# Moving small VectorE and GpSimd steps to other hooks of a Strassen-Winograd block kernel, and one row's load ahead of other transfers

## The chip, the cores and the metric

The kernel runs on one core of one Trainium2 chip. The metric is device time in microseconds (us) of one execution; the figure of a kernel is the median of its runs. TensorE (PE) multiplies matrices into PSUM, VectorE (DVE), ScalarE (ACT) and GpSimd (POOL) do the elementwise work, and SyncE (SP) issues most transfers. Each engine works through its own queue in the order in which the program issued the instructions, and waits on semaphores for the others.

## The reference

The input `x` is 2 x 2048 x 512 in float32, with one condition vector of 512 for each of the two batches. Cut to what matters:

```python
emb = jnp.dot(jax.nn.silu(t), ada_w) + ada_b
shift_msa, scale_msa, gate_msa, shift_mlp, scale_mlp, gate_mlp = jnp.split(emb, 6, axis=-1)
norm = _ln(x) * (1.0 + scale_msa[:, None]) + shift_msa[:, None]
h = jax.nn.gelu(jnp.dot(norm, ssm_w1) + ssm_b1, approximate=False)
x = x + gate_msa[:, None] * (jnp.dot(h, ssm_w2) + ssm_b2)
norm2 = _ln(x) * (1.0 + scale_mlp[:, None]) + shift_mlp[:, None]
hf = jax.nn.gelu(jnp.dot(norm2, ff_w1) + ff_b1, approximate=True)
x = x + gate_mlp[:, None] * (jnp.dot(hf, ff_w2) + ff_b2)
```

`_ln` is a layer norm without weights. `ssm_w1` and `ssm_w2` are 512 x 512, `ff_w1` is 512 x 1024, `ff_w2` is 1024 x 512. There are two residual branches, and each is two matrix products.

## The kernel before, in words

**Tiling.** The 4096 tokens are cut into 8 blocks of 512 tokens (blocks 0 to 3 are the first batch, 4 to 7 the second). A block `x_i` lies in SBUF as 128 partitions of 4 tokens (`C = 4`) with 512 features each, so most elementwise instructions are 128x512.

**Products.** Each block needs the products hA (first layer of the ssm branch), oA (its second layer), hC (first layer of the feed-forward branch, in two groups 0 and 1) and oC (its second layer). Each is done as seven products of half-size quarters, P1 to P7, in the form of Strassen and Winograd: sums of quarters of both operands are made beforehand (`sums_of_first`, `sums_of_second`, lines 212 to 215 and 222 to 225), and the results are put together in three PSUM tiles, the banks y, x and v. P1, P6, P7 and P4 accumulate in y, P2 in x, P5 and P3 in v. After each product VectorE reads what has been accumulated so far, into `s1`, `u2` and `s5` for a first layer (lines 452 to 466; the gelu follows on ScalarE, lines 447 and 470), or straight into the residual `x` for a second layer (line 498). The next product that accumulates in the same bank has to wait for that read. The usual order is

```python
ORDER = ("P1", "P2", "P6", "P5", "P7", "P3", "P4")
```

hA_0 has an order of its own, P1, P2, P5, P6, P3, P7, P4, and oA_0 and hA_1 have `FIRST`, which is P1, P2, P5, P6, P7, P3, P4.

**Hooks.** There is no scheduler: the queue of each engine is the order in which the Python code runs. `group` (line 272) issues the matmuls of a product, then what `after` does with it, then the operations hooked to that product:

```python
            for op in hooks.get(p, ()):
                op()
```

`hook(hooks, places, ops)` hangs the n-th operation on the n-th place, and all further ones on the last place. Which product an operation is hooked to thus settles what stands before and behind it in the queue of its engine.

**The steps that the change touches.** A layer norm is, per token, `bn_stats` and `bn_aggr` on VectorE (lines 324 and 325, one pair for each of the four c), then eight small instructions on GpSimd that make `rstd` and `nmr` (`scales`, lines 333 to 351), then four ScalarE instructions (`normal`, line 364). The result must be turned, features to partitions: blocks 0 and 1 do it with TensorE transposes (`pt`, line 393), the later ones with four VectorE transposes of 32x32 blocks (`turn`, line 375) and 16 transfers from SBUF to SBUF (`move`, line 384). Scale and shift of the condition follow on ScalarE (line 407) or VectorE (line 409).

The gates are folded into the second weights: `make_gate` puts a gate row on all partitions of a PSUM tile (`pgate`, line 201), and `weight_of_second` multiplies `w2` (4 instructions) or `fw2` (8 instructions) by it on VectorE (line 255), with four sums on GpSimd behind them. In `fold2(lo, hi)` the numbers 0 to 3 are the folds of `w2`, and 4 to 7 are its sums. The second bias is multiplied by the gate (`gb2_0`, line 641, and for the second batch line 517) and added to `x` by GpSimd in four instructions (`biases`, line 510). The bias row itself comes by a transfer that SP issues (`load_row`, line 122), 256 KB since it is copied to all 128 partitions, into one of two buffers.

**Around the change.** In the first group (hA_0, oA_0, hA_1) the weights are folded while the first products run. At the batch switch, in block 3 of the loop, the gate of the feed-forward branch is made anew for batch 1 (`refold5`). In the last block but one (`early`, i = 6) oA_7 is put ahead of the second group of hC_6, and the norm of block 7 (`norm_2`) is hooked to the products of that group.

Of the kernel before, what the change touches and what calls it, by code (L numbers as in the profile page):

```python
# [43 lines left out]
def kernel(  # L44
# [16 lines left out]
    nc = tc.nc  # L61
# [9 lines left out]
    PER_B = N // TB  # L71
# [49 lines left out]
    def load_row(t, row):  # L121
        nc.sync.dma_start(out=t, in_=row.unsqueeze(0).to_broadcast([P, D]))
        return t
# [23 lines left out]
    b2_bc = work.tile([P, D], F32, tag="gb", name="gb2_0", bufs=2)  # L147
# [34 lines left out]
    def rows_of_gates(g):  # L182

        pa = ps_g.tile([P, D], F32, tag="x", name=f"pada_{g}")
        for k in range(KD):
            nc.tensor.matmul(
                pa[k * G : (k + 1) * G, :],
                silu[:, k, :],
                ada[g][:, k, :],
                start=True,  # L190
                stop=True,
                tile_position=(0, k * G),
            )
        r = work.tile([P, D], F32, tag="grows", name=f"grows_{g}", bufs=2)
        nc.vector.tensor_tensor(r, pa, brows[:, (2, 5).index(g), :], ALU.add)
        gate_rows[g] = r
# [105 lines left out]
    def hook(hooks, places, ops):  # L302

        for n, op in enumerate(ops):
            hooks.setdefault(places[min(n, len(places) - 1)], []).append(op)
# [201 lines left out]
    def biases(i, gb):  # L507

        return [
            lambda c=c: nc.gpsimd.tensor_tensor(xs[i][:, c, :], xs[i][:, c, :], gb, ALU.add)  # L510
            for c in range(C)
        ]

    def gate_bias(g, b, row, name):

        t = load_row(work.tile([P, D], F32, tag="gb", name=name, bufs=2), row)
        return t, lambda: nc.vector.tensor_tensor(t, gate[g, b], t, ALU.mult)

    def store(i, half):
        s = slice(half * C // 2, (half + 1) * C // 2)  # L520
        nc.sync.dma_start(out=out_blk[i][:, s, :], in_=xs[i][:, s, :])
# [38 lines left out]
    def run(ops):  # L560
        for op in ops:
            op()
# [4 lines left out]
    n1 = {0: Norm(0, 1), 1: Norm(1, 1)}  # L567
# [61 lines left out]
    n1_sums = n1[0].summed(nc.vector)  # L629
# [3 lines left out]
    gb, hA = {2: b2_bc}, {}  # L633
# [9 lines left out]
    def fold2(lo, hi):  # L643
        return [lambda k=k: found["w2"][1][k]() for k in range(lo, hi)]

    hooks = {}
    hook(hooks, ("P1",), n1_sums[2:3])
    hook(hooks, ("P2",), [lambda: rows_of_gates(2)] + n1_sums[3:])
    st = n1[1].stats()
    hook(hooks, ("P5",), [ssm_gate] + fold2(0, 2))  # L650
    hook(hooks, ("P6",), [gb2_0] + biases(0, b2_bc) + fold2(2, 7))
    hook(hooks, ("P3", "P3", "P7"), st)
    hook(hooks, ("P7",), [lambda: modulation(3, 0)])
    hA[0] = First(0, n1[0].ops, hooks, ("P1", "P2", "P5", "P6", "P3", "P7", "P4"))
    w2_ops = found["w2"][0]
# [2 lines left out]
    hooks = {}  # L658
# [5 lines left out]
    st = n2[0].stats()  # L664
# [1 line left out]
    residual("oA_0", 0, hA[0], w2_ops, KD // 2, hooks, order=FIRST)  # L666
    fw1_ops, fw1_sums = weight_of_first("fw1", fw1_sb)
    run(fw1_sums)
    run(n1[1].summed(nc.vector))

    hooks = {}
    hook(hooks, ("P1",), st[2:] + [n2[0].scales])
    hook(hooks, ("P2",), [lambda c=c: n2[0].normal(c, on_pe=True) for c in range(C)])
    hook(hooks, ("P2",), biases(1, gb[2]))
    hook(hooks, ("P6",), [lambda: rows_of_gates(5)])
    hook(hooks, ("P3", "P3", "P4", "P4"), n2[0].turned((1, 3)))
    hA[1] = First(1, n1[1].ops, hooks, FIRST)
# [12 lines left out]
    def fold5(lo, hi):  # L690
        return [lambda k=k: found["fw2"][1][k]() for k in range(lo, hi)]
# [11 lines left out]
    for i in range(NBLK):  # L703
        nxt, nx2, last = i + 1 < NBLK, i + 2 < NBLK, i + 1 == NBLK
        if nx2:
            n1[i + 2] = Norm(i + 2, 1)

        hooks = {} if i else first_hooks
        if nxt:
            hook(hooks, EARLY if i else ("P2",), hA[i + 1].summed(nc.gpsimd))  # L710
        if nx2:
            hook(hooks, ("P2", "P3", "P4"), n1[i + 2].stats())
        if fold:
            hook(hooks, ("P5", "P7"), fold[:2])
        hC = Second(i)
        hC.group(0, n2[i].ops, hooks)

        def second_group(hooks):

            if nx2:  # L720
                hook(hooks, ("P1",), [n1[i + 2].scales])
                hook(hooks, EARLY, [lambda c=c: n1[i + 2].normal(c) for c in range(C)])
                hook(hooks, ("P7", "P3", "P3", "P4"), [lambda c=c: n1[i + 2].turn(c) for c in range(C)])
                hook(hooks, ("P4",), [n1[i + 2].move])
            if i == 0:
                hook(hooks, ("P1", "P2", "P6", "P5"), fold5(4, 8))
                hook(hooks, ("P7",), fold5(8, 12) + [gb5_0] + biases(0, gb[5]))
            if fold:
                hook(hooks, EARLY, fold[2:6])
            hC.group(1, n2[i].ops, hooks)  # L730

        def ssm_residual(hooks):

            if nx2:
                hook(hooks, ("P7",), n1[i + 2].moved())
            if fold:
                hook(hooks, EARLY, fold[6:8])
                hook(hooks, ("P7",), fold[8:])
            n2[i + 1] = Norm(i + 1, 2)
            st = n2[i + 1].stats()  # L740
            hook(hooks, ("P3", "P4"), st[:2] if early else st)
            late_stats.extend(st[2:] if early else ())
            residual(f"oA_{i + 1}", i + 1, hA[i + 1], w2_ops, KD // 2, hooks)

        def norm_2(hooks, turns, then):

            hook(hooks, ("P1",), late_stats + [n2[i + 1].scales])
            hook(hooks, ("P1",), [lambda c=c: n2[i + 1].normal(c) for c in range(C)])
            hook(hooks, turns, [lambda c=c: n2[i + 1].turn(c) for c in range(C)])
            hook(hooks, (then,), [n2[i + 1].move])  # L750


        early = nxt and not nx2
        late_stats = []
        hooks = {}
        hook(hooks, EARLY, hC.summed(0, nc.gpsimd))
        if early:
            ssm_residual(hooks)
            hooks = {}
            norm_2(hooks, ("P6", "P6", "P5", "P7"), "P7")  # L760
        second_group(hooks)
        if i == 0:
            fw2_ops = found["fw2"][0]
        hooks = {}
        hook(hooks, ("P1", "P1", "P1", "P2") if early else EARLY, hC.summed(1, nc.gpsimd))
        if nx2:
            ssm_residual(hooks)
            hooks = {}
        elif not nxt:
            for p in EARLY:  # L770
                run(hooks.get(p, ()))
            hooks = {}
        fold = None

        if nx2:
            norm_2(hooks, ("P2", "P2", "P6"), "P6")
        if i + 3 < NBLK:
            hook(hooks, ("P6",), [lambda: load_x(i + 3)])
        refold2 = (i + 2) % PER_B == 0 and nx2
        if refold2:  # L780
            b = (i + 2) // PER_B
            gb[2], multiply_2 = gate_bias(2, b, b2, f"gb2_{b}")
            hook(hooks, ("P1",), [lambda: load_w("w2", w2, w2_sb)])
        if nx2:
            if refold2:
                hook(hooks, ("P1",), [lambda: make_gate(2, b)])
                hook(hooks, ("P6",), [multiply_2])
            hook(hooks, ("P1", "P2"), n1[i + 2].summed(nc.gpsimd))
            hook(hooks, ("P6",) if refold2 else ("P2", "P6"), biases(i + 2, gb[2]))
        if nxt:  # L790
            hook(hooks, ("P5" if early else "P3",), n2[i + 1].moved())
        if early:
            hook(hooks, ("P7", "P7", "P3", "P3"), n2[i + 1].summed(nc.vector))
        hook(hooks, ("P3",), [lambda: store(i, 0)])
        residual(f"oC_{i}", i, hC, fw2_ops, KH // 2, hooks, last)
        if not last:
            store(i, 1)
        if nx2:
            run(n2[i + 1].summed(nc.gpsimd))

        refold5 = (i + 1) % PER_B == 0 and nxt
        if refold5:
            b = (i + 1) // PER_B
            gb[5], multiply = gate_bias(5, b, fb2, f"gb5_{b}")
            load_w("fw2", fw2, fw2_sb)
            make_gate(5, b)
            fw2_ops, fold = weight_of_second(fw2_sb, fw2_s, gate[5, b], (nc.vector,))
        hooks = {}
        if refold5:
            hook(hooks, ("P6",), [multiply])  # L810
        if nxt:
            hook(hooks, ("P6",) if refold5 else EARLY, biases(i + 1, gb[5]))
        if refold2:
            w2_ops, w2_fold = weight_of_second(w2_sb, w2_s, gate[2, b], (nc.vector,))
            hook(hooks, ALL, w2_fold)
        if nx2:
            hA[i + 2] = First(i + 2, n1[i + 2].ops, hooks)
        else:
            for p in ORDER:
                run(hooks.get(p, ()))  # L820
# [45 lines left out]
```

## Time and profile before

| | us |
|---|---|
| median of 3 runs | 621.32 (619.77 to 621.38) |
| the profiled execution, whole | 618.58 |
| its span, first to last instruction | 616.8 |
| TensorE busy | 603.8 (98%) |
| VectorE busy | 299.3 (49%) |
| ScalarE busy | 173.6 (28%) |
| GpSimd busy | 343.6 (56%) |

The granted clock of TensorE was 1.000 throughout. A line of the timeline or of a group gives start and length in us, engine, source line, operation and operands (out<-in); in brackets is the time for which the engine had been idle, and what ended it. Starts count from the first instruction of the span. A line of the waits gives the engine that waited and the tile it was about to write, with its source line, the instruction waited for, the sum of the waits in us, how many there were and the longest. TensorE's busy time takes in pipelining, so a group of 8 matmuls is shown with 1.89 us and the next one starts 1.73 us after it. The profiled execution is one of several, so its own time is the one that steps in the trace add up to.

### The profile page before, as it was taken

To read this page: it belongs to the slowest core of one execution; us is meant where nothing else is said; L and a number is where in the kernel's file an instruction comes from. 1 tells how busy PE (TensorE), PEld (TensorE's weight loads), DVE (VectorE), ACT (ScalarE), POOL (GpSimd) and SP (SyncE) were. 2 spreads that over 40 slices of the span, in tenths; PEclk is the share of its full clock that TensorE was granted. 3 is DMA by queue.
4 is the path that set the end of the run, shared out by engine and by line. 5 is a ranking of instruction groups with operands and counts; after the bars stand their busy time and mean duration, and the time that the engine had idled before them with its cause. 6 is when DMAs were issued, how large, how long until landed. Compare 5 with 4: busy or idle time off the path is not lost.

```text
span 616.8 us, 7847 instructions
## 1 busy us (share of the span) xinstructions
PE 603.8 (98%) x2899; PEld 523.3 (85%) x2899; DVE 299.3 (49%) x512; ACT 173.6 (28%) x259; POOL 343.6 (56%) x360
## 2 busy tenths in 40 slices
PE   6999999999999999999999999999999999899997
PEld 4777888888888888888888888888888888788886
DVE  4967775335552355534653357533555233714321
ACT  2233341142331431332421334214233141220110
POOL 2696489765543853539637466966654394160330
PEclk9999999999999999999999999999999999999999
DMA  8962002240113302360021820224011400021001
GB/s 323 413 254 69 1 8 62 56 149 1 33 37 95 111 1 69 94 180 17 2 68 39 241 81 13 56 56 149 1 43 27 131 7 2 0 69 68 1 2 69
DMA packets 22075, 47.74 MB, mean 77 GB/s; under 512 B 4068, under 2 KB 4624, under 8 KB 21140
## 3 DMA queue, kind: packets, MB, share of 16 engines
q1 hardware_dynamic: 21952, 47.20, 24.4%
q8 instruction: 23, 0.38, 0.3%
q14 instruction: 16, 0.13, 0.1%
q10 hardware_dynamic: 84, 0.03, 0.0%
HBM read 25.20 MB, written 8.39 MB: 54 GB/s over the span
## 4 chain that ended last, share of the span: by engine, by line
PE 89%; DMA 3%; DVE 3%; POOL 2%; issue 1%; ACT 1%; SPq 0%; DVEq 0%; POOLq 0%; ACTq 0%
PE py_oC L287 18%; PE py_hC L287 17%; PE pv_oC L287 9%; PE pv_hC L287 9%; PE py_oA L287 9%; PE py_hA L287 6%; PE pv_oA L287 5%; PE px_oC L287 4%; PE px_hC L287 4%; PE pv_hA L287 3%; PE px_oA L287 2%; DMA ada<-in_L_cond_ada_w_dram 2%; PE px_hA L287 1%; DMA gb<-in_L_cond_ff_b_dram 1%; PE pt L393 1%
## 5 line engine op out<-in xcount | busy, mean ns | idle before, releaser
L407 ACT ACTIVATE nT<-nT,mod,mod 128x512 f32<-128x512 f32 x52 | 38.1, 802 | 171.7 <-DMA nT<-blocks 159.7
L510 POOL TENSOR_TENSOR x<-x,gb 128x512 f32<-128x512 f32 x64 | 79.2, 1269 | 7.8 <-issue 4.4
L212 POOL TENSOR_TENSOR hSC<-hClo 128x512 f32<-128x512 f32 x16 | 20.4, 1273 | 84.6 <-ACT hClo L447 84.6
L287 PE MATMUL py_hC<-nS,fw_s 128*128 128x256 f32 x256 | 60.5, 379 | 0.0
L287 PE MATMUL py_oC<-fw_s,hSC 128*128 128x256 f32 x256 | 57.9, 379 | 0.0
L364 ACT ACTIVATE nT<-x,nmr,rstd 128x512 f32<-128x512 f32 x52 | 38.7, 803 | 58.5 <-POOL nmr L351 58.5
L498 DVE TENSOR_TENSOR x<-py_oC,x 128x512 f32<-128x512 f32 (+1 forms) x36 | 22.8, 633 | 65.6 <-PE py_oC L287 65.1
L287 PEld LDWEIGHTS py_oC<-fw_s,hSC 128*128 128x128 f32 x256 | 48.7, 190 | 6.5
L287 PEld LDWEIGHTS py_hC<-nS,fw_s 128*128 128x128 f32 x256 | 48.7, 190 | 6.5
L222 POOL TENSOR_TENSOR nS<-nT 128x512 f32<-128x512 f32 x12 | 15.3, 1273 | 62.2 <-ACT nT L407 49.9
L324 DVE BATCH_NORM_STATS2 st<-x 128x6 f32<-128x512 f32 x64 | 43.2, 674 | 5.6 <-DMA x<-in_x_dram 5.4
L333 POOL TENSOR_SCALAR ve<-mv 128x4 f32<-128x4 f32 x16 | 4.0, 247 | 68.0 <-DVE mv L325 61.3
L375 DVE STREAM_TRANSPOSE blocks<-nT 128x512 f32<-128x512 f32 x52 | 34.0, 688 | 3.5 <-ACT nT L364 3.5
L498 DVE TENSOR_TENSOR x<-py_oA,x 128x512 f32<-128x512 f32 x32 | 22.1, 691 | 26.0 <-PE py_oA L287 24.4
L287 PE MATMUL pv_hC<-nT,fw_s 128*128 128x256 f32 x128 | 30.3, 380 | 1.6 <-DVE s5hC L461 1.6
L287 PE MATMUL py_hA<-nS,w_s 128*128 128x256 f32 x128 | 30.4, 381 | 0.4 <-DVE u2hA L458 0.4
L287 PE MATMUL py_oA<-w_s,hSA 128*128 128x256 f32 x128 | 30.3, 380 | 0.0
L287 PE MATMUL py_hC<-nT,fw 128*128 128x256 f32 x128 | 30.2, 379 | 0.0
L287 PE MATMUL pv_hC<-nT,fw 128*128 128x256 f32 x128 | 30.2, 379 | 0.0
L287 PE MATMUL py_hC<-nS,fw 128*128 128x256 f32 x128 | 30.2, 379 | 0.0
L287 PE MATMUL px_hC<-nT,fw 128*128 128x256 f32 x128 | 30.2, 379 | 0.0
L287 PE MATMUL pv_oC<-fw,hClo 128*128 128x256 f32 x128 | 28.9, 379 | 0.0
(147 smaller groups left out, 1230.5 us busy)
## 6 DMA issues: line engine op xcount, KB each, us to landing
nT<-blocks SPq DMA_DIRECT2D x208, 64.0 KB, 2.0
out_dram<-x SPq DMA_DIRECT2D x15, 512.0 KB, 7.3
x<-in_x_dram SPq DMA_DIRECT2D x7, 1024.0 KB, 6.8
ada<-in_L_cond_ada_w_dram SPq DMA_DIRECT2D x6, 1024.0 KB, 11.4
fw<-in_L_cond_ff_w_dram SPq DMA_DIRECT2D x3, 2048.0 KB, 14.9
w<-in_L_cond_ssm_w_dram SPq DMA_DIRECT2D x3, 1024.0 KB, 6.4
x<-in_x_dram SPq DMA_DIRECT2D x2, 512.0 KB, 5.0
gb<-in_L_cond_ssm_b_dram SPq DMA_DIRECT2D x2, 256.0 KB, 12.7
```

Of the source, the lines that this page charges most:

```text
L212: lambda: eng.tensor_tensor(s[1], q["11"], q["21"], ALU.subtract),
L222: lambda: eng.tensor_tensor(s[1], q["22"], q["12"], ALU.subtract),
L287: nc.tensor.matmul(ps[b][j * apart][:, j, :], lhs(p, j, k), rhs(p, j, k), start=(fresh and j * (not apart) == 0 and k == 0), stop=(p in (" ...
L324: nc.vector.bn_stats(st, xs[self.i][:, c, :])
L333: v.tensor_scalar(ve, self.mv[:, :, 1], EPS, None, ALU.add)
L364: nc.scalar.activation(t, x_c, AF.Identity, bias=self.nmr[:, c : c + 1], scale=self.rstd[:, c : c + 1])
L375: nc.vector.transpose(self.bl[:, :, :, c, :].rearrange("p m k q -> p k m q"), self.nT[:, c, :].rearrange("p (k m q) -> p k m q", k=KD, m=C),)
L393: nc.tensor.transpose(pt[:, c * P : (c + 1) * P], self.xn[:, c, k * P : (k + 1) * P], ident)
L407: nc.scalar.activation(dst, src, AF.Identity, bias=shift, scale=scale)
L498: nc.vector.tensor_tensor(d, ps[BANK[p]][:, js], d, ALU.add)
L510: lambda c=c: nc.gpsimd.tensor_tensor(xs[i][:, c, :], xs[i][:, c, :], gb, ALU.add)
```

## The change

Four places are edited.

1. hA_0: `gb2_0` and the four bias adds of block 0 go from P6 to P5, ahead of the first fold; one fold goes from P5 to P6. Of the four pairs of statistics of block 1, two were hooked to P3 and two to P7; now one is hooked to P3 and three to P7.
2. hA_1: the fourth sum of the operand of hA_1 (line 225, VectorE) was issued ahead of P1, now it is hooked to P5.
3. The batch switch: the row of `fb2` for the second batch is loaded ahead of oC_3 and no longer after it. On SP the issue is now between the block moves of x_5 and those of x_4, and was after the stores of block 3.
4. Block 6: the four turns of the norm of block 7 were hooked to P6, P6, P5 and P7 of the second group of hC_6, now to P7, P3, P3 and P4; the moves follow at P4 and no longer at P7.

```diff
-    hook(hooks, ("P5",), [ssm_gate] + fold2(0, 2))
-    hook(hooks, ("P6",), [gb2_0] + biases(0, b2_bc) + fold2(2, 7))
-    hook(hooks, ("P3", "P3", "P7"), st)
+    hook(hooks, ("P5",), [ssm_gate, gb2_0] + biases(0, b2_bc) + fold2(0, 1))
+    hook(hooks, ("P6",), fold2(1, 7))
+    hook(hooks, ("P3", "P7"), st)
...
-    run(n1[1].summed(nc.vector))
+    n1_sums = n1[1].summed(nc.vector)
+    run(n1_sums[:3])
...
     hook(hooks, ("P2",), biases(1, gb[2]))
+    hook(hooks, ("P5",), n1_sums[3:])
...
-            norm_2(hooks, ("P6", "P6", "P5", "P7"), "P7")
+            norm_2(hooks, ("P7", "P3", "P3", "P4"), "P4")
...
         hook(hooks, ("P3",), [lambda: store(i, 0)])
+        refold5 = (i + 1) % PER_B == 0 and nxt
+        if refold5:
+            b = (i + 1) // PER_B
+            gb[5], multiply_5 = gate_bias(5, b, fb2, f"gb5_{b}")
         residual(f"oC_{i}", i, hC, fw2_ops, KH // 2, hooks, last)
...
-        refold5 = (i + 1) % PER_B == 0 and nxt
         if refold5:
-            b = (i + 1) // PER_B
-            gb[5], multiply = gate_bias(5, b, fb2, f"gb5_{b}")
             load_w("fw2", fw2, fw2_sb)
             make_gate(5, b)
...
-            hook(hooks, ("P6",), [multiply])
+            hook(hooks, ("P6",), [multiply_5])
```

## The prediction

> **What bounds the kernel now.** The page's first two lines say that TensorE bounds it: it is busy for 603.8 of 616.8 us, and no other engine for more than 56%.
>
> ```profile
> span 616.8 us, 7847 instructions
> PE 603.8 (98%) x2899; PEld 523.3 (85%) x2899; DVE 299.3 (49%) x512; ACT 173.6 (28%) x259; POOL 343.6 (56%) x360
> ```
>
> So time can only come out of TensorE's own idle stretches. The chain of waits, kept to PE, lists every one; those from 20 us on are:
>
> ```profile
> PE pv_hC L287 <- DVE s5hC L461: 1.6, 1, 1.6
> ...
> PE pv_oA L287 <- POOL r L335: 1.4, 1, 1.4
> ...
> PE py_hA L287 <- DVE s5hA L463: 0.9, 1, 0.9
> PE py_hA L287 <- DVE u2hA L458: 0.4, 1, 0.4
> PE pv_hA L287 <- DVE s5hA L461: 0.4, 1, 0.4
> PE pt L393 <- ACT blocks L364: 0.3, 1, 0.3
> ```
>
> These are single waits, 5.0 us together, and all lie where the change puts its hand: four at 29 to 61 us, one at 354 us, one at 537 us. The timeline then shows what stood ahead of each releaser on VectorE. First group:
>
> ```profile
> 27.41 0.68 DVE L324 BATCH_NORM_STATS2 st<-x 128x6 f32<-128x512 f32 x1
> ...
> 28.23 0.66 DVE L324 BATCH_NORM_STATS2 st<-x 128x6 f32<-128x512 f32 x1
> 28.93 0.18 DVE L325 BATCH_NORM_AGGREGATE mv<-st 128x2 f32<-128x6 f32 x1
> 29.03 0.66 DVE L463 TENSOR_TENSOR s5hA<-py_hA,s5hA 128x512 f32<-128x512 f32 x1
> ...
> 34.17 1.10 DVE L212 TENSOR_TENSOR hSA<-hA 128x512 f32<-128x512 f32 x1
> 35.77 0.69 DVE L213 TENSOR_TENSOR hA<-hA 128x512 f32<-128x512 f32 x1 [0.49 <-issue]
> ```
>
> P7 of hA_0 ended at 27.83, but L463, which must read the y bank before P4 may write it, stood behind two statistics. The wait put down to `r` L335 I read otherwise: P5 of oA_0 reads hA's quarter 21, which L213 rewrites; L213 ended at 36.46, PE started at 36.61. The two later places:
>
> ```profile
> 352.75 0.69 DVE L517 TENSOR_TENSOR gb<-pgate,gb 128x512 f32<-128x512 f32 x1 [1.77 <-DMA gb<-in_L_cond_ff_b_dram]
> 353.36 0.68 DVE L461 TENSOR_TENSOR s5hA<-pv_hA,colsT 128x512 f32<-128x512 f32 x1
> ...
> 535.19 1.42 DVE L375 STREAM_TRANSPOSE blocks<-nT 128x512 f32<-128x512 f32 x2 [2.19 <-ACT nT L364]
> 536.53 0.65 DVE L461 TENSOR_TENSOR s5hC<-pv_hC,colsT 128x512 f32<-128x512 f32 x1
> ```
>
> In both, an instruction that waits for something slow holds L461, and PE's P3 waits for L461 to free the v bank.
>
> **What the Trainium skill says.** "PSUM — Partial Sum Buffer", section Engine vs sequencer instructions: the queues of VectorE, ScalarE and GpSimd are strict FIFO. The trace agrees: L461's input was complete at 533.93, yet it ran at 536.53, after two turns. "SBUF — State Buffer", section Who interferes with whom: a VectorE instruction with two SBUF inputs and a GpSimd instruction that reads SBUF lock each other out. The trace agrees: L212 began at 34.17 while POOL's L224 ran until 34.73, and took 1.10 instead of 0.69 us. The same page, The DMA setup-cost knee, fits a transfer as 2 us plus its bytes at 436 GB/s, an estimate of 2.6 us for a 256 KB row; the trace has 7.4 us behind the stores at 345 us and 12.7 us in the loaded start, so I use those.
>
> **The change part by part.** A fed group of 8 matmuls starts 1.73 us after the last one, the first after a stall 1.83. No instruction is added or removed, on any engine; only places change.
>
> *A, hA_0.* One pair of statistics goes from P3 to P7. L463 then follows the first pair, at 28.23, and P4 starts at 28.94 instead of 29.74: 0.80 us. All four pairs still end at 31.29, since they only swap with L463. `gb2_0` goes ahead of the first fold, at 22.69, where the gate is ready (PE ended it at 22.65); its row, issued at 8.86, landed 12.7 us later, at 21.56. Fold 0 slips by 0.60 into the 0.44 us that VectorE waited at 24.41 and into the place of the fold that moves to P6, so P6's u2 stays at 24.41 and the last fold ends at 26.90 as before. GpSimd's four bias adds come from 25.84 to 23.5 and end at 28.4; its three L222 to L224 end at 32.4 instead of 34.7, the scales (3.1 us without being held, as at 55.05) at about 35.5 to 36.3 instead of 39.1. Behind them L225 and the 9.7 us of fw1 sums end at 46.6 to 47.4 instead of 50.0; fw1 landed at 34.1 and is needed at 36.9.
>
> P5 of oA_0: P1 starts at 28.94+1.83 = 30.77, so P5 is due at 34.23. VectorE adds P1 at 32.77 (its end at 32.66, plus 0.11 as before), L212 follows at 33.37 and L213 at 34.10, ending 34.79; PE starts 0.15 later, at 34.94. Now GpSimd runs only scales there instead of L224. Not held at all: 34.94; held like before (0.41 in L212, 0.49 ahead of L213): 35.84. I take 35.05, as only short operations of 128x4 remain. So the shift at P5 is 36.61-35.05 = 1.56 us (0.77 to 1.67), the first 0.80 in it: a shortened wait, which stays L213's.
>
> *B, hA_1.* L222 on VectorE took 1.05 us while fw1's last sum ran on GpSimd; now it starts at 47.96, after that sum: 0.36 sooner than the shift. L225 leaves the place ahead of s1 and comes back ahead of u2 L458, so L458 gains nothing by it: it starts when L225 is done, at 54.00, and PE's P7 goes at 54.74, where 54.64 was possible. Before, P6 was 0.14 and P7 0.45 late: 0.49 gained (0.1 to 0.59). The last two statistics of oA's result no longer stand behind L225, so scales, ScalarE's four normals and the transposes behind them come about 0.6 us sooner still than TensorE: the normals end at 58.4, the fourth transpose is due at 58.6, and its 0.50 us (4 transposes ahead of P4 took 1.38 instead of 0.88) goes (0.2 to 0.5). First group in all: 1.56+0.49+0.50 = 2.55.
>
> *C, the switch.* The row of fb2 is issued between the two sets of 16 block moves on SP, at about 319, and SP then waits until 332.40 anyway. The row's other buffer was last read by bias adds that ended at 284.8, so SP isn't held, and fw2's load behind it is not later. L517 runs after u2 at 350.9, L461 on time at 351.99. P3 at 353.54 and no restart: 0.66 us (P4 at 355.93 becomes 355.27). The bias adds start 1.3 us sooner, which nobody waits for.
>
> *D, block 6.* L461 runs at 534.0, L463 at 535.7, the turns at 536.3, 538.05, 538.7 and 539.3. P3 starts at 535.50: P4 at 539.07 becomes 537.23, 1.84 us. What is later: the 16 moves on SP start at 540.0 instead of 539.0, and so end some 2.8 us later by TensorE's clock; ScalarE modulates at 552.4 to 555.4. Next, L222 at P7 of oC_6 is due on VectorE at 557.1, so 1.7 us cover it; if they go, only that queue slips, and hC_7 at 563.1 has 7.7 us.
>
> Sum: 2.55+0.66+1.84 = **5.05 us**, from 3.4 (0.77+0.1+0.2+0.55+1.74) to 5.3. The profiled execution, 618.58 us with 1.78 us around its span, becomes 613.5. It lies 2.7 below the median of the runs, 621.32, and runs are what is compared: 621.32-5.05 = **616.3**.
>
> **The rivals.** *A's wait only changes its face:* L212 and L213 are held by GpSimd as before and B's u2 stays late, so the first group gives 0.77+0.1+0.2, and the sum is about 3.5: 617.8. For it: L213 had 0.49 us of idle that no view explains. Against: the one long neighbour, L224, is gone from there. *D does not do it:* in the built program L461 now waits for ScalarE as well as PE, a wait that the turn ahead of it used to cover. Were it for the normals or the gelu behind them (537.8), P3 would stay late: 3.2 us, 618.1. Against: with four temporaries the buffer's last reader is the gelu at 513.98. *Slower, by gb2_0:* the whole of VectorE's queue now stands behind the row of b2 from 22.69 on, with DMA full at 410 GB/s. Past some 0.4 us of cover each microsecond of a later landing delays u2, P7 and P4 by one. It cancels the change when the row lands at 28.2 and makes it slower by over 0.3% from about 30, 8.5 us later than here; 623.2 and more then. The 1.1 us in hand speak against it.
>
> **How the numbers follow.** Forecast 0.72; the first rival 0.12, the second 0.08, the slower one 0.03, unnamed troubles 0.05. A measurement can tell about 0.3%, 1.9 us, from no change; the first three cases are all beyond that, but runs before spread by 1.6 us. Faster 0.87, same 0.08, slower 0.05. The range goes from 5.3 below the lowest run, less some scatter, to the two rivals with the spread on top: 614.0 to 619.5.
>
> **What would show it.** In the profile after, the chain of waits on PE should have no wait for L461 at all, none for `blocks` L364, about 0.2 for L463 and 0.7 to 0.8 ahead of pv_oA; POOL's bias adds start at 23.5, L517 without a wait for DMA, hC_0 starts at 61.8. Wrong would be a DMA wait at L641, L461 with a wait for ACT, a wait at hC_7's first groups, or a pv_oA wait of over 1.4 us.

## The result and the profile after

| us | before | after |
|---|---|---|
| median of 6 runs each, side by side | 620.62 (619.50 to 621.44) | 613.37 (613.20 to 614.73) |
| ratio, with its 95% interval | | 0.9888 [0.9873, 0.9904] |
| the profiled execution, whole | 618.58 | 613.35 |
| its span | 616.8 | 611.6 |

The changed kernel is faster by 1.1%. Its profiled execution lies 5.2 us below that of before, where the prediction's sum was 5.05; its median lies 7.2 us below the median of before, and below the predicted range. Both have to be explained. The first lines of the page after show the same work on each engine in a shorter span (the two instructions more are on none of the engines counted):

```profile
span 611.6 us, 7849 instructions
PE 604.3 (99%) x2899; PEld 524.6 (86%) x2899; DVE 300.9 (49%) x512; ACT 173.5 (28%) x259; POOL 343.6 (56%) x360
```

The chain of waits of the changed kernel, kept to PE, is complete in three lines (engine and tile that waited, what it waited for, sum, count, longest):

```profile
PE pada L164 <- DMA ada<-in_L_cond_ada_w_dram: 1.4, 1, 1.4
PE idle L585 <- POOL ident masks.py:199: 1.3, 1, 1.3
PE pv_oA L287 <- POOL rstd L349: 1.0, 1, 1.0
```

Of the six waits shown before, five are gone, and 1.0 us is left ahead of P5 of oA_0. The timeline of VectorE after shows that place; this execution's start-up was 0.54 us quicker (`pada` at 11.74, before 12.28), so 0.54 must be added to compare with before:

```profile
26.87 0.68 DVE L324 BATCH_NORM_STATS2 st<-x 128x6 f32<-128x512 f32 x1
27.58 0.18 DVE L325 BATCH_NORM_AGGREGATE mv<-st 128x2 f32<-128x6 f32 x1
27.68 0.66 DVE L463 TENSOR_TENSOR s5hA<-py_hA,s5hA 128x512 f32<-128x512 f32 x1
...
32.22 0.69 DVE L498 TENSOR_TENSOR x<-py_oA,x 128x512 f32<-128x512 f32 x1 [0.33 <-POOL ve L333]
32.83 0.68 DVE L212 TENSOR_TENSOR hSA<-hA 128x512 f32<-128x512 f32 x1
34.01 0.69 DVE L213 TENSOR_TENSOR hA<-hA 128x512 f32<-128x512 f32 x1 [0.50 <-issue]
```

L463 now follows one pair of statistics and not two. L212 no longer overlaps one of GpSimd's 128x512 sums and takes 0.68 us instead of 1.10. But the 0.50 us of idle ahead of L213 is still there. Further on, at the switch and in block 6, L461 runs as soon as TensorE lets it ("<-PE pv_hA", "<-PE pv_hC"):

```profile
348.17 0.68 DVE L517 TENSOR_TENSOR gb<-pgate,gb 128x512 f32<-128x512 f32 x1
349.29 0.69 DVE L461 TENSOR_TENSOR s5hA<-pv_hA,colsT 128x512 f32<-128x512 f32 x1 [0.44 <-PE pv_hA L287]
...
530.66 0.69 DVE L461 TENSOR_TENSOR s5hC<-pv_hC,colsT 128x512 f32<-128x512 f32 x1 [1.03 <-PE pv_hC L287]
532.92 0.70 DVE L375 STREAM_TRANSPOSE blocks<-nT 128x512 f32<-128x512 f32 x1
534.65 1.89 DVE L375 STREAM_TRANSPOSE blocks<-nT 128x512 f32<-128x512 f32 x3
```

The 5.2 us between the two spans add up by place: 0.54 at the start-up; 2.19 from there to the start of hC_0 (64.34 before, 61.61 after, less the 0.54); L461's waits of 0.4 and 1.6 us with the restarts behind them at the switch and in block 6 for the rest, 2.5. The 0.54 is no effect of the change, since nothing moved lies so early. So this pair of traces gives the change some 4.7 us, and its 5.2 match the prediction's 5.05 in part by luck. Runs of the parts have to settle it.

### The profile page after: what moved, and what is told of

It is laid out like the page before. It is cut to its first block, busy times and chain, and to the rows that moved or that the text cites. A ratio compares the mean times of both kernels' runs of the same rounds, so it can differ in the third digit from the quotient of the medians.

```text
span 611.6 us, 7849 instructions
## 1 busy us (share of the span) xinstructions
PE 604.3 (99%) x2899; PEld 524.6 (86%) x2899; DVE 300.9 (49%) x512; ACT 173.5 (28%) x259; POOL 343.6 (56%) x360
## 4 chain that ended last, share of the span: by engine, by line
PE 96%; DMA 2%; DVE 1%; POOL 0%; issue 0%; SPq 0%
PE py_oC L287 18%; PE py_hC L287 18%; PE pv_oC L287 9%; PE pv_hC L287 9%; PE py_oA L287 9%; PE py_hA L287 9%; PE pv_oA L287 5%; PE px_hC L287 5%; PE px_oC L287 5%; PE pv_hA L287 4%; PE px_hA L287 2%; PE px_oA L287 2%; DMA ada<-in_L_cond_ada_w_dram 2%; PE pt L393 1%; PE pgate L201 1%; DVE st L324 0%
## 5 line engine op out<-in xcount | busy, mean ns | idle before, releaser
L212 POOL TENSOR_TENSOR hSC<-hClo 128x512 f32<-128x512 f32 x16 | 20.3, 1271 | 83.4 <-ACT hClo L447 83.4
L498 DVE TENSOR_TENSOR x<-py_oC,x 128x512 f32<-128x512 f32 (+1 forms) x36 | 22.8, 632 | 63.8 <-PE py_oC L287 63.3
L222 POOL TENSOR_TENSOR nS<-nT 128x512 f32<-128x512 f32 x12 | 15.3, 1274 | 62.2 <-ACT nT L407 61.1
L498 DVE TENSOR_TENSOR x<-py_oA,x 128x512 f32<-128x512 f32 x32 | 22.1, 690 | 23.7 <-PE py_oA L287 21.8
L287 PE MATMUL py_oC<-fw,hClo 128*128 128x256 f32 x128 | 28.9, 379 | 0.0
```

What stands on the lines that cost most here:

```text
L212: lambda: eng.tensor_tensor(s[1], q["11"], q["21"], ALU.subtract),
L222: lambda: eng.tensor_tensor(s[1], q["22"], q["12"], ALU.subtract),
L287: nc.tensor.matmul(ps[b][j * apart][:, j, :], lhs(p, j, k), rhs(p, j, k), start=(fresh and j * (not apart) == 0 and k == 0), stop=(p in (" ...
L498: nc.vector.tensor_tensor(d, ps[BANK[p]][:, js], d, ALU.add)
```

## The experiments

**How they are compared.** The kernels were run in three groups, on three chips, each beside the kernel before. Its medians there were 618.63 (51 runs), 618.44 (27) and 618.48 us (11). In one run of before in six or so TensorE's granted clock falls for about 3 us in the first 17, and some runs of the other kernels show the same. Where I take differences of tenths, both sides are runs at the full clock, that is with a mean granted clock of 0.999 or more (medians of before 618.54 and 618.38 in the first two groups). Ratios and medians are over all runs.

**1. Before, once more** (no edit). The question was what the 2.7 us between the profiled execution and the median of before were.

> The kernel before, unchanged: ratio 1.000, and its runs once more spread over about 2 us. Theory R (the row): the profile of before was one short draw of a time that varies, and what varies is when fb2's row lands behind the stores at the batch switch; a second profile then has a wait for L461 near 354 us that differs from 0.4 us, up to 2.9, by as much as its span differs from 616.8. Theory S (the start): what varies lies in the first 65 us, where DMA is full; the second profile then starts hC_0 at another time than 64.34 by as much as its span differs. Theory K (the clock): the spans differ where a granted clock under 1.000 is listed, and the waits do not differ.

Measured: 618.49 us (13 runs, 618.08 to 621.35), ratio 1.0003 [0.9989, 1.0017]. Before is a kernel of 618.5 us, as its profiled execution had said; the 621.32 was the uncommon figure. The profiled execution of this repeat took 619.54 us, with a span of 617.8, and shows how one run of before comes to be longer. First the waits on PE, then SP's issue, then VectorE:

```profile
PE pv_hA L287 <- DVE s5hA L461: 2.1, 1, 2.1
...
PE pv_hC L287 <- DVE s5hC L461: 1.6, 1, 1.6
PE pv_oA L287 <- POOL r L335: 1.4, 1, 1.4
```

```profile
344.66 0.48 SPq L122 DMA_DIRECT2D gb<-in_L_cond_ff_b_dram  x1
```

```profile
353.72 0.69 DVE L517 TENSOR_TENSOR gb<-pgate,gb 128x512 f32<-128x512 f32 x1 [3.43 <-DMA gb<-in_L_cond_ff_b_dram]
```

The row of fb2 was issued at 344.66 and L517 got it at 353.72, 9.1 us later; in the first trace it was 7.4 (345.36 to 352.75). So L517 waited 3.43 us and PE's P3 behind it 2.1, not 0.4. The prediction's price of C came from the quicker of the two. The wait grew by 1.7 us and the span by 1.0 only, since the start was 0.7 quicker (hC_0 at 63.64, before 64.34): theory R and a part of S. The clock of theory K shows in three other runs of this repeat, at 620.1 to 621.4 with a mean of 0.997.

**2 to 4. The switch and block 6, each alone, and everything but the switch.**

```diff
 # 2: before, with only this of the change
+        if refold5:
+            b = (i + 1) // PER_B
+            gb[5], multiply_5 = gate_bias(5, b, fb2, f"gb5_{b}")
         residual(f"oC_{i}", i, hC, fw2_ops, KH // 2, hooks, last)
...
 # 3: before, with only this of the change
-            norm_2(hooks, ("P6", "P6", "P5", "P7"), "P7")
+            norm_2(hooks, ("P7", "P3", "P3", "P4"), "P4")
 # 4: after, with the edit of 2 undone
```

> Before, with only the row of fb2 loaded sooner (part C). Step C of the prediction: 0.66 us less, ratio 0.9989. Theory R: 2 to 3 us less, ratio 0.995 to 0.997, and runs that lie within 0.5 us of each other. Theories S and K: 0.66 us less and the spread of before.

> Before, with only the turns of block 7's norm moved (part D). Step D of the prediction: 1.84 us less, ratio 0.9970, no wait for L461 at 537 us. Theory R: the same 1.84 us, with the spread of before. Theory K: more than 1.84 us, if fewer idle stretches of TensorE keep its clock up.

> The changed kernel with the row of fb2 loaded where it was before (part C undone). Prediction's steps: 620.6 less 4.4 us, 616.2, and 0.66 us over the changed kernel. Theory R: 2 to 3 us over the changed kernel (615.5 to 616.5) and spread over some 2 us. Theory S: within 0.7 us of 614.1 and not spread.

| | median, us (runs) | ratio to before | at the full clock |
|---|---|---|---|
| 2: the row alone | 617.34 (21) | 0.9982 [0.9972, 0.9992] | 617.31: 1.23 under before |
| 3: block 6 alone | 616.92 (22) | 0.9978 [0.9967, 0.9989] | 616.68: 1.86 under before |
| 4: all but the row | 614.67 (5) | 0.9936 [0.9917, 0.9954] | 1.3 over the changed kernel's 613.37 in the first comparison (it was not run in this group) |

Block 6 gives what was predicted, 1.86 for 1.84. The row gives 1.23 or 1.3, twice the predicted 0.66, and less than the 2 to 3 of theory R; kernel 4's expected 616.2, reckoned from 620.6 for before, missed by 1.5. The two kernels here that keep the late row show why the price was too low; these are their waits on PE for L461 at the switch, kernel 3 first and then kernel 4:

```profile
PE pv_hA L287 <- DVE s5hA L461: 0.7, 1, 0.7
```

```profile
PE pv_hA L287 <- DVE s5hA L461: 0.9, 1, 0.9
```

From SP's issue to L517 it took 7.7 and 7.9 us there. Of the five traces with the late row (kernel 6 below is the fifth) the first one had the shortest landing, and the wait follows the landing: 0.4, 0.7, 0.9, 1.3 and 2.1 us for 7.4, 7.7, 7.9, 8.3 and 9.1. Issued early, the row landed after 3.4 us in the changed kernel and 3.3 in kernel 2, long before L517. Kernel 2's runs at the full clock lie within 1.0 us (617.17 to 618.14), those of before within 2.3 (617.88 to 620.16).

The profiled execution of kernel 2 was one with a low clock. A table of stretches of it (stretch; length, busy time and count of PE, PEld, DVE, ACT, POOL; granted clock; DMA share; GB/s):

```profile
9.00:12.00 3.00, 1.38 (x42) 1.14 (x46) 2.01 (x8) 1.52 (x2) 0.58 (x1) 0.98 1.05 396
12.00:15.00 3.00, 3.00 (x40) 2.62 (x29) 0.48 (x2) 0.41 (x1) 0.63 (x1) 0.50 1.05 403
15.00:18.00 3.00, 3.00 (x19) 2.79 (x19) 2.37 (x3) 1.15 (x2) 2.84 (x3) 0.95 1.05 407
```

and the same stretches of the changed kernel:

```profile
9.00:12.00 3.00, 1.52 (x44) 1.10 (x47) 2.02 (x9) 1.52 (x2) 0.64 (x1) 1.00 1.05 394
12.00:15.00 3.00, 3.00 (x51) 2.75 (x41) 1.54 (x4) 1.46 (x2) 0.58 (x1) 1.00 1.05 406
15.00:18.00 3.00, 3.00 (x15) 2.47 (x13) 2.86 (x4) 0.10 (x1) 2.84 (x3) 1.00 1.05 410
```

At 12 to 15 us TensorE ran at half its clock (0.50) in one and at 1.00 in the other, and hA_0's P6 then began at 23.96 and at 21.94 us: 2 us lost before the first instruction that the change moves. This fits the Trainium skill, "TensorE: Matmul & The Clock Gate", section What's actually happening: the clock is halved unless recent activity releases it, and activity is judged in windows of 3413 ns that run free of the kernel's start. In both traces TensorE is busy for only half of 9 to 12 us, so one window may or may not count as idle. Kernels 6 and 10 have traces with the same fall (0.52 and 0.51). The other eleven traces stay at 1.00, with TensorE busy for no more of 9 to 12 us (1.30 to 1.55 us, against 1.35 to 1.42 in the three). The page speaks of a whole idle window; the waits here are shorter (1.4 us ahead of `pada`), and no run moved them, so the cause is argued and only the cost is shown. The changed kernel has such runs too (614.73 in the first comparison and 615.34 in kernel 12, both at a mean clock of 0.997), so the change doesn't gain by avoiding them.

**5 and 6. After, once more (no edit), and the first group alone** (before, with edits 1 and 2 of the change).

> The changed kernel, unchanged, beside many runs of the kernel before. Theory M (the mixture): the steps were right, 5.2 us in all, and the recorded ratio of 0.9888 came from runs of before that had the early stretch of lower clock, which costs 2 us, or a late row. Then runs at full clock are at 613.4 here against 618.5, ratio 0.991 to 0.992, and the changed kernel has low-clock runs too, at 615.3, in about one run of six. Rival F (the change keeps the clock up): no low-clock runs in the changed kernel, and a ratio near 0.989.

> Before, with only the edits of the first group (A and B). Prediction's steps: 2.55 us less at full clock, 616.0. By the trace of the changed kernel against e3 it should be 2.2 us less, 616.3. The wait at pv_oA is 1.0 us as in the changed kernel, those for L463, L458 and blocks are gone, and hC_0 starts 2.2 us sooner after the second pada than in before.

Measured: 613.21 us (4 runs, 613.11 to 613.26), ratio 0.9910 [0.9897, 0.9923]; and 616.53 (22 runs), 0.9975 [0.9963, 0.9986], at the full clock 616.37, which is 2.0 under before and what the traces had led to expect. The parts now add up: 2.0 + 1.23 + 1.86 = 5.1 us, and 618.38 - 613.21 = 5.2. To about 0.1 us, neither a gain nor a loss comes from doing them together. None of kernel 5's four runs has a low clock; against rival F speak the two of the changed kernel named above and the ratio, which did not come back to 0.989.

**7 and 9. Each half of the edit in hA_0 undone** (after, with these lines back).

```diff
 # 7: the statistics back
-    hook(hooks, ("P3", "P7"), st)
+    hook(hooks, ("P3", "P3", "P7"), st)
 # 9: the gate row, the bias adds and the fold back
-    hook(hooks, ("P5",), [ssm_gate, gb2_0] + biases(0, b2_bc) + fold2(0, 1))
-    hook(hooks, ("P6",), fold2(1, 7))
+    hook(hooks, ("P5",), [ssm_gate] + fold2(0, 2))
+    hook(hooks, ("P6",), [gb2_0] + biases(0, b2_bc) + fold2(2, 7))
```

> The changed kernel with the statistics of block 1 hooked as before (two to P3, two to P7); the bias adds stay ahead. By the prediction's first step P4 of hA_0 starts 0.80 us later, and since L213 and all behind it follow P4's gelu and P1, the whole 0.8 us is lost: 614.2 at full clock. Rival: L213 is held by something that does not come with P4 (GpSimd's scales), then P5 of oA_0 starts when it does in the changed kernel and nothing is lost: 613.4.

> The changed kernel with gb2_0, the bias adds and the fold back at P6 as before; the statistics stay moved. The prediction gave the bias adds no time of their own beyond an unheld L213 and 0.36 us at L222: 613.7 to 614.3 at full clock. If VectorE and GpSimd lock each other out wherever both read SBUF, then L224 again holds L212 (34.2 us or so), fw1's last sum, ending near 48.8, holds L222 by about 1 us and u2 L458 makes PE wait: 614.5 to 615.5. Rival: the bias adds were moved for nothing, 613.2.

Measured: 615.48 us (5 runs), ratio 0.9946 [0.9933, 0.9959], 2.3 over the changed kernel of the same group, for the statistics (the 614.2 expected missed); 614.66 (6 runs), 0.9925 [0.9902, 0.9949], 1.3 over kernel 12 below, for the bias adds, as expected if the engines lock each other out. The halves cost 3.6 us when each is taken away alone, though the whole first group is worth 2.0: each depends on the other. Kernel 7 shows how. The 0.8 us that L463 is late comes back as predicted, and then VectorE's next sums meet GpSimd's long ones. PE's waits, VectorE and GpSimd:

```profile
PE pv_oA L287 <- POOL nmr L350: 1.0, 1, 1.0
PE py_hA L287 <- DVE s5hA L463: 0.9, 1, 0.9
PE py_oA L287 <- DVE x L498: 0.9, 1, 0.9
...
PE py_oA L287 <- DVE hSA L214: 0.2, 1, 0.2
```

```profile
36.02 1.66 DVE L214 TENSOR_TENSOR hSA<-hA 128x512 f32<-128x512 f32 x1
37.78 2.66 DVE L215 TENSOR_TENSOR hSA<-hA,hSA 128x512 f32<-128x512 f32 x1
```

```profile
35.86 1.27 POOL L225 TENSOR_TENSOR w_s<-w,w_s 128x512 f32<-128x512 f32 x1
37.08 2.81 POOL L212 TENSOR_TENSOR fw_s<-fw 128x1024 f32<-128x1024 f32 x1
```

L214 took 1.66 us and L215 2.66, where L214 takes 0.68 and L215 1.57 in the changed kernel; L215 ended at 40.44, half a microsecond after GpSimd's sum of 128x1024. Behind it stands L498, for which P7 waited 0.9 us. This is the lock that the prediction cited ("SBUF — State Buffer", section Who interferes with whom), at a place where it did not look. Which of the two begins first decides who is held. In the changed kernel L214 began 0.12 us ahead of GpSimd's L225 and ran at full speed, and it was L225 that took longer:

```profile
35.22 0.68 DVE L214 TENSOR_TENSOR hSA<-hA 128x512 f32<-128x512 f32 x1
```

```profile
35.34 1.70 POOL L225 TENSOR_TENSOR w_s<-w,w_s 128x512 f32<-128x512 f32 x1
```

In kernel 7, 0.8 us later on VectorE, L225 began 0.16 us ahead of L214, took 1.27 us, and L214 was held. A held sum of 128x512 on VectorE ended 0.54 or 0.55 us after GpSimd's instruction did, in nine such pairs in the traces of before, after, 7, 8, 9 and 11, however long it had been held. In kernel 9 the same happens at P5 of oA_0, where L213 falls beside L224, as L212 did before, and P5 waits 1.5 us, and in hA_1, where L222 falls beside a sum of fw1:

```profile
PE pv_oA L287 <- POOL ve L333: 1.5, 1, 1.5
...
PE py_hA L287 <- DVE u2hA L458: 0.6, 1, 0.6
```

```profile
48.09 1.65 DVE L222 TENSOR_TENSOR nS<-nT 128x512 f32<-128x512 f32 x1 [1.07 <-ACT nT L407]
```

```profile
46.84 2.36 POOL L215 TENSOR_TENSOR fw_s<-fw,fw_s 128x1024 f32<-128x1024 f32 x1
```

**8. The wait ahead of pv_oA, tested.** The view names GpSimd's `rstd` as the releaser; the prediction read it as L213. Here L212 and L213 go ahead of the L498 of P1, and GpSimd's work stays as it is (after, with this edit).

```diff
-    hook(hooks, ("P1",), [n1[1].scales] + fold2(7, 8) + hA_sums[:2])
+    run(hA_sums[:2])
+    hook(hooks, ("P1",), [n1[1].scales] + fold2(7, 8))
```

> The changed kernel with the first two sums for oA_0 (L212, L213 on VectorE) ahead of P1's addition to x (L498) instead of behind it. If pv_oA's wait of 1.0 us is for L213, as the prediction read it, and not for GpSimd's rstd, as the view of waits names it, then P5 of oA_0 starts 0.6 to 1.0 us sooner: 612.4 to 612.8 at full clock. If it is for GpSimd, nothing changes: 613.4. If L498 itself, now later, holds PE's P6 or P7: slower than 613.4.

Measured: 612.96 us (4 runs, 612.96 to 612.97), ratio 0.9906 [0.9893, 0.9919]: 0.25 us under the changed kernel of the same group (613.11 to 613.26), the fastest of all, though not quite the 612.4 to 612.8 expected. L213, PE's P5, and what came instead, on VectorE and on GpSimd:

```profile
32.51 0.69 DVE L213 TENSOR_TENSOR hA<-hA 128x512 f32<-128x512 f32 x1
...
46.52 1.55 DVE L222 TENSOR_TENSOR nS<-nT 128x512 f32<-128x512 f32 x1 [1.08 <-ACT nT L407]
```

```profile
33.60 1.89 PE L287 MATMUL pv_oA<-w,hA 128*128 128x256 f32 x8
```

```profile
45.17 2.36 POOL L215 TENSOR_TENSOR fw_s<-fw,fw_s 128x1024 f32<-128x1024 f32 x1
```

P5 runs at 33.60 without a wait, while `rstd` ends later still (36.04, and 34.76 in the changed kernel). So the releaser is L213, and the named one is wrong. The gain of some 1.1 us there is mostly given back in hA_1: L222 being 1.2 us earlier, and GpSimd's sums 0.4 us later, L222 now overlaps GpSimd's last fw1 sum (45.17 to 47.53) and takes 1.55 us instead of 0.69, and P7 waits 0.6 us for the u2 behind it.

**10 and 11. The edit in hA_1 undone, and taken one product further on top of 8.**

```diff
 # 10: after, with the fourth sum ahead of P1 again
-    n1_sums = n1[1].summed(nc.vector)
-    run(n1_sums[:3])
+    run(n1[1].summed(nc.vector))
...
-    hook(hooks, ("P5",), n1_sums[3:])
 # 11: kernel 8, with the fourth sum at P6
-    hook(hooks, ("P5",), n1_sums[3:])
-    hook(hooks, ("P6",), [lambda: rows_of_gates(5)])
+    hook(hooks, ("P6",), n1_sums[3:] + [lambda: rows_of_gates(5)])
```

> The changed kernel with part B undone (L225 of hA_1's operand ahead of P1 again). By the prediction the normals come 0.6 us later and the fourth transpose waits for them again by 0.5 us, L458 stands where it stood: 613.7 at full clock. Rival: all of what B seemed to give came from A's GpSimd work being over sooner, then 613.2.

> The kernel of e8, with L225 of hA_1's operand behind u2 L458 (hooked to P6) and no longer ahead of it (P5). In e8 TensorE gained 1.2 us at P5 of oA_0 and gave 0.7 back at P7 of hA_1, where it waited 0.6 us for L458, late since fw1's last sum on GpSimd held L222. With 0.6 us less ahead of L458 the wait should go: 612.3 to 612.5, the fastest of all. If the wait is for something else: 612.96.

Measured: 613.78 us (6 runs), ratio 0.9910 [0.9885, 0.9936], for 10, and 613.34 (6 runs), 0.9915 [0.9888, 0.9941], for 11, beside kernel 12's 613.33. Undoing the edit in hA_1 costs about 0.5 us, and 11 gains nothing; its expectation missed. In 11 the wait for u2 at P7 is gone, and one for the normals of oA_0's result stands in its place. PE's wait for them, kernel 10 first, then 11:

```profile
PE pt L393 <- ACT blocks L364: 0.3, 1, 0.3
```

```profile
PE pt L393 <- ACT blocks L364: 0.4, 1, 0.4
```

The transposes of hA_1 are the next limit: TensorE can be made earlier in oA_0, but ScalarE's normals, fed by statistics and scales that follow oA_0's last read, come no earlier. In 11 they even come 0.33 us later than in 8 (they start at 55.37 and at 55.04), since the sum that was moved again, L225 on VectorE, now falls beside one of the scales on GpSimd, L347, which takes 0.64 us and not 0.20:

```profile
53.43 0.68 DVE L225 TENSOR_TENSOR nS<-nT,nS 128x512 f32<-128x512 f32 x1
```

```profile
53.53 0.64 POOL L347 TENSOR_TENSOR e<-e,ve 128x4 f32<-128x4 f32 x1
```

The transposes start 0.6 us sooner than in 8 (57.12, 57.72), but P4 behind them 0.32 later (58.95, 58.63). So what 8 had won is lost there.

**12. After, a third time** (no edit), beside 9, 10 and 11.

> The changed kernel a third time, to see what the kernel before does in another session. Theory M: 613.2 to 613.4 against 618.4 to 618.6, ratio 0.991. If the kernel before lies at 620 here at full clock, then a session shifts it (the landing of fb2's row), and 0.989 was such a session.

Measured: 613.33 us (6 runs, 613.14 to 615.34), ratio 0.9911 [0.9885, 0.9936]. The median of the changed kernel moved by 0.16 us over three comparisons (613.37, 613.21, 613.33), that of before by 2.2 (620.62, then 618.63, 618.44, 618.48). Of kernel 12's six runs, the one of 614.38 at a mean clock of 1.000 stays unexplained.

## Why the prediction was right and where it was wrong

**The step that failed** is the one from the profiled execution to the median: "runs are what is compared: 621.32-5.05 = 616.3". It took the 2.7 us by which before's median stood above its profiled execution for something that the changed kernel would have too. The changed kernel doesn't: median 613.37, profiled 613.35. Nor does before have it as a rule: over 89 further runs its medians were 618.4 to 618.6, and its profiled 618.58 was right. From the profiled execution the sum gave 613.5, 0.2 us off. That it came so near is luck in part: the first group gave 2.0 us for 2.55 and the switch 1.23 for 0.66, and the two errors cancel. But the range was drawn around the wrong base, and the result fell out of it at the bottom.

**Why the first runs of before lay high** is settled only in part. Two causes are shown that lengthen single runs: the clock at 12 to 15 us, about 2 us, which hits both kernels; and a late landing of the fb2 row, which cost 1.7 us more in repeat 1 than in the first trace (waits of 2.1 and 0.4) and which the change removes for good. Three of those six runs at 621.3 to 621.4 would need both, three at 619.5 to 619.9 the second alone. Other runs fit this: at a mean clock of 0.996 or 0.997, kernels with the early row lay 1.4 to 2.3 us above their median at the full clock, those with the late row up to 3.9. But of the six themselves no traces are kept, and it is not shown. So the 7.2 us of the first comparison hold some 2 us that are no steady effect: the later comparisons give 5.2 (613.21 against 618.44) and 5.15 (613.33 against 618.48).

**A, hA_0: the order right, one term too large.** P4 came 0.80 us earlier, as predicted (29.74 to 28.40, of which 0.54 is start-up). GpSimd's bias adds were due at 23.5, and started at 22.97 + 0.54 = 23.51. P5 came 1.22 us earlier, where 1.56 was taken and 0.77 the lower bound. L498 and L212 started at 32.76 and 33.37 on before's clock, to 0.01 as worked out; L213, due at 34.10, started at 34.55. The failing term is "I take 35.05, as only short operations of 128x4 remain". It counted the 0.49 us of idle ahead of L213 as GpSimd's doing, and let it go with L224. The idle stayed, and 1.0 us of wait at P5 with it, where 0.7 to 0.8 was forecast. GpSimd doesn't set it: L213 starts 0.49 to 0.51 us after L212's end in all twelve traces that have the two sums at P1, whatever GpSimd runs. In kernel 9 GpSimd's L224 goes on through the whole of the idle, and L213 starts before it ends; what L224 does there is to make L213 long.

```profile
32.69 0.68 DVE L212 TENSOR_TENSOR hSA<-hA 128x512 f32<-128x512 f32 x1
33.86 1.18 DVE L213 TENSOR_TENSOR hA<-hA 128x512 f32<-128x512 f32 x1 [0.49 <-issue]
```

```profile
32.78 1.71 POOL L224 TENSOR_TENSOR w_s<-w 128x512 f32<-128x512 f32 x1
```

In kernels 8 and 11, where the two sums stand ahead of L498, L213 follows L212 after 0.10 us. So the idle goes with the place in VectorE's queue, and some 0.4 us of kernel 8's gain at P5 is this. What makes it is open. The reading that L213 and not GpSimd releases P5 is shown by kernel 8.

**B, hA_1: right in its sum.** From P5 of oA_0 to hC_0 the trace lost 0.97 us (27.73 before, 26.76 after), for 0.99. Of it about 0.5 is the moved sum itself (kernel 10); the rest, L222 free of GpSimd's sum, comes from A. All of the first group: 2.19 us in the trace, 2.0 in kernel 6, for 2.55; hC_0 so began at 62.15 on before's clock, and not at 61.8, and the 0.2 us expected for L463 stayed away.

**C, the switch: right in kind, half the size.** 1.23 to 1.3 us instead of 0.66, because one trace's landing of 7.4 us was taken as the usual one. The bounds worked out for C had no spread of landings in them at all; a term that hangs on a transfer needed one, upwards here.

**D, block 6: right**, 1.86 for 1.84. What was to be late next has cover: ScalarE's modulation waited for the moves and ended at 551.73; VectorE's L222, which stands behind an L498 in its queue, used the result at 553.64, 1.9 us later (1.7 predicted).

```profile
548.80 2.93 ACT L407 ACTIVATE nT<-nT,mod,mod 128x512 f32<-128x512 f32 x4 [12.19 <-DMA nT<-blocks]
```

**The rivals.** Of the first, the idle ahead of L213 did stay (0.50 us), but L212 was no longer held, and the idle is not GpSimd's. D was not held by L461's added wait for ScalarE: it waited for PE alone. The row of b2 landed in time, since the bias adds began as predicted.

## What to carry to other kernels

When a profiled execution and a median differ, repeat the kernel before you add the difference to a forecast: the offset is a property of some runs, and the parts of it that hang on a transfer may go with the very change that is forecast. Price a step that waits for a transfer by several landings, since one trace shows one of them. Where VectorE and GpSimd share the sums, lay their 128x512 instructions side by side before and after every shift in time, and see which begins first: 0.8 us of lateness cost 2.3 here, and 1.1 us won in one product became 0.25 at the end.

## What the hardware showed beyond expectation

- TensorE's clock fell to 0.50 for some 3 us at 12 to 15 us in about one run in six (14 of the 89 runs of before had a lowered mean clock), at a cost of some 2 us.
- A 256 KB row issued on SP behind the stores took 7.4, 7.7, 7.9, 8.3 and 9.1 us to be usable in five traces of the same transfer; issued among the block moves it landed after 3.3 and 3.4 us.
- A VectorE sum of 128x512 from two SBUF operands takes 0.68 us alone. Begun while a GpSimd sum ran, it ended 0.54 or 0.55 us after that one, in nine pairs, and so took up to 2.66 us (beside a sum of 128x1024). Begun first, it took 0.68, and GpSimd's sum of 128x512 took 1.70 us instead of 1.27.
